# The first loads of a spline-built feed-forward layer: two sets of control points asked for by ScalarE, and x asked for behind the first set and its table

## The chip, the cores and the metric

One core of a Trainium2 chip runs the whole program. TensorE (PE, with its weight loads PEld), VectorE (DVE), ScalarE (ACT) and GpSimd (POOL) compute; SyncE (SP) here only asks for transfers. Each engine works through its own instructions in the order in which they were built, and stops at an instruction whose semaphores have not been reached. Transfers are asked for by an instruction on an engine's queue and then done by 16 DMA engines. The metric is the device time of one execution in microseconds (us).

## The reference

The input x is 4 sequences of 512 rows with 512 columns. Three steps follow each other: a feed-forward layer, an attention layer with a recurrent state, and the same feed-forward layer again. Only the first concerns the change. Its three weight matrices are not inputs: each is interpolated from a short vector of control points.

```python
def spline_reconstruct(control_points, out_size, in_size):
    n = out_size * in_size
    idx, f = _catmull_rom_grid(control_points.shape[0], n)
    p0, p1, p2, p3 = (control_points[idx[0]], control_points[idx[1]], control_points[idx[2]], control_points[idx[3]])
    ...
    w = 0.5 * (2.0 * p1 + (p2 - p0) * f + (2.0 * p0 - 5.0 * p1 + 4.0 * p2 - p3) * f2 + (3.0 * p1 - p0 - 3.0 * p2 + p3) * f3)
    return w.reshape(out_size, in_size)
gate_w = spline_reconstruct(gate_cp, INTER, HIDDEN)      # 2048 x 512
up_w = spline_reconstruct(up_cp, INTER, HIDDEN)          # 2048 x 512
down_w = spline_reconstruct(down_cp, HIDDEN, INTER)      # 512 x 2048
gate = jnp.einsum('bsh,ih->bsi', hidden_states, gate_w)
up = jnp.einsum('bsh,ih->bsi', hidden_states, up_w)
inter = jax.nn.silu(gate) * up
return jnp.einsum('bsi,hi->bsh', inter, down_w)
...
x = x + 0.5 * _L0_ffn_ref(_layernorm(x, axis=-1), ...)
x = x + _L0_attn_ref(_layernorm(x, axis=-1), ...)
x = x + 0.5 * _L0_ffn_ref(_layernorm(x, axis=-1), ...)
```

## The kernel before

The kernel never builds the dense weights. A row of a weight is piecewise cubic, so it keeps a small set of coefficients (`wc` for gate and up, `wr`, `we` and `cm` for down) and multiplies them with features of x. The first call of `ffn` (L299) has two pieces of work at its start that do not depend on each other:

- **Features of the first sequence.** `load` (L331) brings x, 1 MB, into the tile `ffn_x`. `whole` (L384) normalizes it: statistics on VectorE (`ln_st`, `ln_mv`, `ln_var`), the power -0.5 on GpSimd (`ln_rstd`, L346), the scaled rows on VectorE (`ln_xn`, L361). TensorE turns them (`ln_pt`, L368), ScalarE copies them (`ffn_xnT`, L369), TensorE multiplies them with the table `lag` (`pf`, L374), and ScalarE copies the eight results (`ft`, L378).
- **Coefficients.** `spline_weights` (L655) reads control points into the windows `win`: for each of gate, up and down 16 transfers of overlapping rows (L676), 6.5 KB each for gate and up, 3.1 KB for down. It also loads two tables of 1.5 MB (`tab`, L679 and L684) and constants (`shift`, `node`, `post`, `postd`, `rest`, `postr`, `sel`, `side`). `gate_up` (L712) first selects rows (`wr`, L707 and L709; one instruction covers gate and up together), then multiplies with the first table (`pr`, L719: gate's four on VectorE, up's four on GpSimd), and VectorE adds (`cf`, L720). TensorE turns the sums (`cf_pt`, L725), ScalarE copies them (`nat`, L726), and three engines permute them into `cfT` (L731). `down` (L741) does the like with the second table (`pr` L749, `cfd` L750, `cf_pt` L753, `natd` L755) and permutes into `cfTd` with 32 small copies on GpSimd (L766).

Then comes `hidden` (L427) for the first sequence: 16 products for gate (`pg`) and 16 for up (`pu`, L439). The coefficients are finished on the way, by `block` (L769): every second step a pair of `pw` products (L777) from `cfT`, a copy (L780) and a predicated copy (L781) into `wc`, and at every step `pwd` products (L789) from `cfTd` and a small table `rw` that SyncE brings. `pw`, `pwd`, `pwe`, `pf`, `ln_pt` and `cf_pt` share two PSUM buffers. Two further sequences are loaded meanwhile (`ffn_x`, L608 and L615) and their statistics taken.

In this part nothing fixes the order of the work by hand. The tile framework orders each engine's instructions when the kernel is built, from its own estimates of when each will be ready; so a moved transfer can change the order on other engines too. The later parts (`by_hand`, L604, and the attention) are ordered by hand.

All transfers except GpSimd's gathers of `hid` (L458) are asked for by SyncE, in one queue. The framework gives the completion of transfers eight semaphores in turn: an instruction that asks for a transfer waits until the transfer eight places earlier, on the same semaphore, has landed.

The lines that set the order of the first asks are L398 and L399 (x, then `lag`), then, inside `spline_weights`, `shift`, gate's 16, the first table, up's 16, down's 16, and the constants.

Of the kernel before, what the change touches and what calls it, by code (L numbers as in the profile page):

```python
# [19 lines left out]
P = 128  # L20
# [31 lines left out]
G_LAG = G_NODE + NG_F * 2 * P  # L52
G_POST = G_LAG + NC * NG_F * NODES
# [211 lines left out]
def tile_macaron(ctx, tc, x, w_qkvz, w_ba, conv_w, dt_bias, a_log, norm_w, w_out, cps, consts, grid, starts, out):  # L265
    nc = tc.nc
# [32 lines left out]
    def ffn(src, dst, build, beside=iter(())):  # L299
        with ExitStack() as st:  # L300
# [3 lines left out]
            io = pool(early, "ffn_io", 2)  # L304
# [4 lines left out]
            ps = pool(late, "ffn_ps", 2, space=PSUM, side="right")  # L309
            py = pool(late, "ffn_py", 1, space=PSUM, side="right")  # L310

            lag = wp.tile([P, NC, NG_F * NODES], F32, name="lag")
            wc = [wp.tile([P, 2, GR], F32, name=f"wc{g}", tag=f"wc{g}") for g in range(NG_F)]
# [17 lines left out]
            def load(b, name, pool):  # L331
                xt = pool.tile([P, NT, H], F32, name=name)
                nc.sync.dma_start(xt, src(b).rearrange("(t p) h -> p t h", p=P))
                return xt
# [49 lines left out]
            def whole(xt):  # L384
                ft, stats, norms, turns, inter = features(xt)
                stats()
                for n_, t_ in zip(norms, turns):
                    n_()
                    t_()
                    tick()  # L390
                drain()
                for f in inter:
                    f()
                    tick()
                drain()
                return ft

            xt = load(0, "ffn_x", io)  # L398
            nc.sync.dma_start(lag.rearrange("p c k -> p (c k)"), grid[:, G_LAG:G_POST])  # L399
            built = ExitStack()  # L400
            if build:
                with ExitStack() as scratch:
                    coefficients, block = spline_weights(built, scratch, wc, ps)
                    ft = whole(xt)
                    for f in coefficients:
                        f()
            else:
                for g in range(NG_F):
                    nc.sync.dma_start(wc[g].rearrange("p m i -> p (m i)"), wg_d[g])
                ft = whole(xt)  # L410
# [16 lines left out]
            def hidden(b, ft):  # L427

                to, box = hid[b % 2], {}

                def gate(k):
                    if build and b == 0:
                        block(k, wr, we, cm)
                    product(k, 0)

                def product(k, m):
                    at = (k % 2) * P
                    pm = box[m] = gu.tile([P, S], F32, name=("pg", "pu")[m], tag="gu")
                    nc.tensor.matmul(pm, wc[k // 2][:, m, at : at + P], ft[k // 2], start=True, stop=True)  # L439
                    if m:  # L440
                        pg = box[0]
                        later(1, lambda: finish(k, pg, pm))

                def finish(k, pg, pu):
                    sg = wk.tile([P, S], F32, name="ffn_sg")
                    nc.scalar.activation(sg, pg, AF.Silu)
                    it = wk.tile([P, S], F32, name="ffn_it", bufs=4)
                    nc.vector.tensor_tensor(it, pu, sg, ALU.mult)  # L448
                    nc.sync.dma_start(to[k * P : (k + 1) * P, :], it)

                return [f for k in range(NB) for f in (lambda k=k: gate(k), lambda k=k: product(k, 1))]
# [155 lines left out]
            if B > 1:  # L607
                xt = load(1, "ffn_x", io)  # L608
                plan["nxt"] = features(xt)
                plan["nxt"][1]()  # L610
            if build:
                first = hidden(0, plan["ft"])
# [39 lines left out]
                    if step is None:  # L652
                        break

    def spline_weights(st, scratch, wc, ps):  # L655

# [8 lines left out]
        win = [c1.tile([P, 2, NB, ext[0]], F32, name="win0"), c1.tile([P, 1, 4, ext[1]], F32, name="win1")]  # L667
        for m in range(3):
            n = m // 2
            r = ext[n] - 9  # L670
            rows = 512 // r

            for q in range(16):
                view = bass.AP(cps[m].tensor, starts[n][q], [[r, rows], [1, ext[n]]])
                first = (q * rows) % P
                nc.sync.dma_start(win[n][first : first + rows, m % 2, q * rows // P, :], view)  # L676
            if m == 0:
                tab = [c1.tile([P, 64 * NF * NJ], F32, name=f"tab{k}", tag=f"tab{k}") for k in range(2)]
                nc.sync.dma_start(tab[0], grid[:, G_TAB[0] : G_TAB[1]])  # L679
        node = sp.tile([64, NG_F, 2, P], F32, name="node")  # L680
        nc.sync.dma_start(node.rearrange("p g e j -> p (g e j)"), grid[:64, G_NODE:G_LAG])
        post = sp.tile([P, INTER // 4], F32, name="post")
# [127 lines left out]
                nc.sync.dma_start(we_d, we)  # L810
                nc.sync.dma_start(cm_d, cm.rearrange("p c h -> p (c h)"))

        return (gate_up, down), block

# [893 lines left out]

    steps = attention()
    ffn(lambda b: x[b], lambda b: x1[b], True, steps)
    for _ in steps:
        pass
    ffn(lambda b: x2[b], lambda b: out[b], False)


# [30 lines left out]
```

## Time and profile before

| | us |
|---|---|
| median of 4 runs | 3772.76 |
| lowest, highest | 3770.35, 3775.47 |
| the profiled execution | 3773.43 |
| its span on the core | 3771.6 |
| PE busy | 3553.8 (94%) |
| DVE busy | 2543.2 (67%) |
| ACT busy | 1469.4 (39%) |
| POOL busy | 866.2 (23%) |

The profile is of one execution. All times in it count from the start of the span. "Busy" sums the instructions of an engine; asking for a transfer and waiting for a semaphore are not counted. In a timeline a line gives the start, the busy time, the engine, the source line, the operation, what it writes and reads, the shapes, and in brackets how long the engine had been idle and what ended that. "SPq" is SyncE's queue of asks. A "DMA" piece in the chain of work is the time from the ask to the landing. The windows table gives for each stretch the busy time of each engine and the clock that TensorE was granted as a share of full speed.

### The profile page before, as it was taken

What the parts mean: (1) busy time and instruction counts of PE and PEld (TensorE: products, weight loads), DVE (VectorE), ACT (ScalarE), POOL (GpSimd) and SP (SyncE); (2) the same over time, 40 slices, a digit from 0 to 9 for tenths busy, and PEclk for the clock granted to TensorE, in tenths of its full rate; (3) what the DMA queues carried; (4) which work ended last, traced back from release to release, by engine and by line L of the source; (5) the groups of instructions that cost most, each with busy time, mean ns of one, the idle gap of its engine ahead of it and who ended that gap; (6) DMA issues with size and microseconds to landing.
All of it is one profiled execution on the core that took longest, in us unless ns stands there. A gap on an engine that the chain in (4) does not pass through costs nothing.

```text
span 3771.6 us, 62529 instructions
## 1 busy us (share of the span) xinstructions
PE 3553.8 (94%) x24568; PEld 1966.2 (52%) x24568; DVE 2543.2 (67%) x5928; ACT 1469.4 (39%) x3440; POOL 866.2 (23%) x655
## 2 busy tenths in 40 slices
PE   5998679999999999999999999999999999987998
PEld 2333245555555555555555556555555555553333
DVE  5223677787777788778777777777778777552321
ACT  2321124444444444444444444444444444443221
POOL 2113112222222222222222222222222221210221
PEclk8999889999999999999999999999999999998999
DMA  4435311212222222122222222222222211203452
GB/s 144 154 131 187 104 47 48 71 58 62 66 70 64 82 64 72 55 60 65 63 60 82 60 71 61 60 61 65 73 82 60 63 52 51 66 22 111 151 199 90
DMA packets 303093, 302.25 MB, mean 80 GB/s; under 512 B 96880, under 2 KB 231312, under 8 KB 302224
## 3 DMA queue, kind: packets, MB, share of 16 engines
q1 hardware_dynamic: 292560, 264.70, 22.6%
q0 software_dynamic: 10240, 33.56, 2.9%
q8 instruction: 194, 3.18, 0.4%
q14 instruction: 99, 0.81, 0.1%
HBM read 247.60 MB, written 50.59 MB: 79 GB/s over the span
## 4 chain that ended last, share of the span: by engine, by line
PE 70%; DVE 15%; POOL 5%; ACT 5%; DMA 3%; issue 2%; SPq 1%; DVEq 0%; POOLq 0%; ACTq 0%
PE pj L1041 15%; PE py L1507 12%; PE pz L1359 9%; DVE acc L1051 4%; PE pks L1398 4%; PE y L492 3%; PE pp L1283 3%; PE pg L439 3%; PE pu L439 3%; PE pos L1436 3%; POOL oo L1480 2%; DVE ee L1227 2%; PE pzz L1423 2%; PE pu L1344 2%; PE pos L1434 2%
## 5 line engine op out<-in xcount | busy, mean ns | idle before, releaser
L1051 DVE SCALAR_TENSOR_TENSOR acc<-pj,cw,acc 128x511 f32<-128x511 f32 (+2 forms) x768 | 574.3, 748 | 188.8 <-ACT acc L1049 170.6
L1041 PE MATMUL pj<-xnT,w_v 128*128 128x512 f32 x1024 | 521.0, 602 | 0.0
L1359 PE MATMUL pz<-w_z,xnT 128*128 128x512 f32 x1024 | 514.2, 614 | 0.0
L1507 PE MATMUL py<-w_o,gT 128*128 128x512 f32 x1024 | 509.5, 611 | 0.4
L448 DVE TENSOR_TENSOR ffn_it<-pu,ffn_sg 128x512 f32<-128x512 f32 x128 | 88.4, 691 | 362.2 <-PE pu L439 250.8
L1041 PE MATMUL pj<-xnT,w_q 128*128 128x512 f32 x512 | 255.9, 603 | 9.4 <-ACT ksq L1112 9.4
L1041 PE MATMUL pj<-xnT,w_k 128*128 128x512 f32 x512 | 247.1, 602 | 3.9 <-DVE acc L1051 3.3
L1415 ACT ACTIVATE tq<-pks,rqe 128x128 f32<-128x128 f32 x384 | 120.0, 363 | 330.5 <-DVE rq L1256 192.5
L1485 ACT ACTIVATE oo<-oo,orr 128x128 f32<-128x128 f32 x512 | 162.6, 389 | 204.6 <-POOL oo L1480 204.6
L1082 POOL TENSOR_TENSOR rsk<-msk,phalf 128x4 f32<-128x4 f32 x64 | 66.8, 1044 | 719.3 <-DVE msk L1080 712.1
L1049 ACT ACTIVATE acc<-pj,cw 128x512 f32<-128x512 f32 x256 | 175.1, 684 | 139.1 <-PE pj L1041 139.1
L1507 PEld LDWEIGHTS py<-w_o,gT 128*128 128x128 f32 x1024 | 170.3, 190 | 107.5 <-issue 96.4
L1359 PEld LDWEIGHTS pz<-w_z,xnT 128*128 128x128 f32 x1024 | 170.3, 191 | 101.4 <-issue 90.4
L1082 POOL TENSOR_TENSOR rsq<-msq,phalf 128x4 f32<-128x4 f32 x64 | 64.9, 1014 | 681.3 <-DVE msq L1080 668.6
L1059 ACT ACTIVATE th<-acc 128x512 f32<-128x512 f32 x256 | 161.7, 632 | 148.2 <-DVE acc L1051 144.1
L1041 PEld LDWEIGHTS pj<-xnT,w_v 128*128 128x128 f32 x1024 | 170.5, 191 | 70.7 <-issue 64.1
L1221 POOL TENSOR_TENSOR ee<-ident,w 128x1024 f32<-128x1024 f32 x64 | 141.3, 2208 | 226.1 <-DVE pT L1292 226.1
L458 POOL DMA_INDIRECT nat<-hid,idx x128 | 122.9, 960 | 299.7 <-PE y_pt L509 104.5
L1473 DVE TENSOR_REDUCE om<-osq 128x4 f32<-128x512 f32 x128 | 87.1, 680 | 153.8 <-ACT osq L1472 153.8
L1166 DVE TENSOR_TENSOR inv<-inv,inv_tmp 128x30 f32<-128x30 f32 (+14 forms) x480 | 168.9, 352 | 16.5
L1479 POOL TENSOR_TENSOR orr<-om,phalf 128x8 f32<-128x8 f32 x64 | 104.9, 1640 | 311.9 <-DVE om L1477 311.9
L1423 PEld LDWEIGHTS pzz<-rr,tt 128*128 128x128 f32 x768 | 114.5, 192 | 114.5 <-DVE rr L1408 49.2
(213 smaller groups left out, 6824.1 us busy)
## 6 DMA issues: line engine op xcount, KB each, us to landing
hid<-ffn_it SPq DMA_DIRECT2D x128, 256.0 KB, 2.1
w_v<-in_L_attn_W_qkvz SPq DMA_DIRECT2D x64, 512.0 KB, 3.6
w_z<-in_L_attn_W_qkvz SPq DMA_DIRECT2D x64, 512.0 KB, 5.1
ab<-decay_c SPq DMA_DIRECT2D x64, 512.0 KB, 3.7
w_o<-in_L_attn_W_out SPq DMA_DIRECT2D x32, 1024.0 KB, 5.6
w_k<-in_L_attn_W_qkvz SPq DMA_DIRECT2D x64, 256.0 KB, 2.8
w_q<-in_L_attn_W_qkvz SPq DMA_DIRECT2D x64, 256.0 KB, 3.2
ad<-decay_b SPq DMA_DIRECT2D x256, 32.0 KB, 2.2
```

The source lines that it names most:

```text
L439: nc.tensor.matmul(pm, wc[k // 2][:, m, at : at + P], ft[k // 2], start=True, stop=True)
L1041: nc.tensor.matmul(pj, w()[:, c, col : col + DK], xnT[:, c, :], start=c == 0, stop=c == NC - 1)
L1049: nc.scalar.activation(acc, pj, AF.Copy, scale=cw[:, ch, 3:4])
L1051: nc.vector.scalar_tensor_tensor(acc[:, d:], pj[:, : S - d], cw[:, ch, 3 - d : 4 - d], acc[:, d:], ALU.mult, ALU.add)
L1059: nc.scalar.activation(th, box["acc"], AF.Tanh)
L1166: nc.vector.tensor_tensor(ee[:, j + 1 :, :j], ee[:, j + 1 :, :j], tj, ALU.add)
L1221: nc.gpsimd.tensor_tensor(ee, id8, bc(s["w"], 3, P), ALU.mult)
L1359: nc.tensor.matmul(pz, xnT[:, c, t * P : (t + 1) * P], pair["wz"][:, c].rearrange("p j k -> p (j k)"), start=c == 0, stop=c == NC - 1,)
L1398: nc.tensor.matmul(pks[:, j].rearrange("p r v -> p (r v)"), m[:, tok], box["state"].rearrange("p r v -> p (r v)"), start=True, stop=True,)
L1423: nc.tensor.matmul(pzz[:, r], s["tT"][:, 2 * t + r], rr[:, r], start=True, stop=True)
L1485: nc.scalar.activation(s["oo"][:, t, r], s["oo"][:, t, r], AF.Copy, scale=s["orr"][:, u : u + 1])
L1507: nc.tensor.matmul(box["py"], pair["gT"][r][:, t, :], pair["wo"][:, r, :], start=r == 0, stop=r == 3)
```

## The change

The load of x and of `lag` becomes a function, `first`. When coefficients are built, `spline_weights` calls it after gate's 16 transfers and the first table have been asked for. The 16 transfers of up and the 16 of down are asked for by ScalarE's queue (`nc.scalar`) in place of SyncE's. In the second call of `ffn`, which builds nothing, `first` is called at the place where the two loads stood.

```diff
-            xt = load(0, "ffn_x", io)
-            nc.sync.dma_start(lag.rearrange("p c k -> p (c k)"), grid[:, G_LAG:G_POST])
+            def first():
+                xt = load(0, "ffn_x", io)
+                nc.sync.dma_start(lag.rearrange("p c k -> p (c k)"), grid[:, G_LAG:G_POST])
+                return xt
+
             built = ExitStack()
             if build:
                 with ExitStack() as scratch:
-                    coefficients, block = spline_weights(built, scratch, wc, ps)
+                    coefficients, block, xt = spline_weights(built, scratch, wc, ps, first)
                     ft = whole(xt)
                     for f in coefficients:
                         f()
             else:
+                xt = first()
...
             for q in range(16):
                 view = bass.AP(cps[m].tensor, starts[n][q], [[r, rows], [1, ext[n]]])
-                first = (q * rows) % P
-                nc.sync.dma_start(win[n][first : first + rows, m % 2, q * rows // P, :], view)
+                at = (q * rows) % P
+                eng = nc.scalar if m else nc.sync
+                eng.dma_start(win[n][at : at + rows, m % 2, q * rows // P, :], view)
             if m == 0:
                 tab = [c1.tile([P, 64 * NF * NJ], F32, name=f"tab{k}", tag=f"tab{k}") for k in range(2)]
                 nc.sync.dma_start(tab[0], grid[:, G_TAB[0] : G_TAB[1]])
+                xt = first()
...
-        return (gate_up, down), block
+        return (gate_up, down), block, xt
```

In the built program the order of instructions differs before the second group's `pw` and nowhere behind it. What moves beside the asks themselves: VectorE and GpSimd select rows and start `pr` ahead of the statistics of x, which stand among the `pr` and `cf` steps; `cfT`'s copy on VectorE stands behind the statistics of the next x; the first `wc` predicate stands behind three `ln_xn` of that x; `pwd`, `pg`, `pwe` and `pu` of the first group stand behind both `pw`; and the first two `rw` are asked for ahead of the first store of `wc`. ScalarE's 32 asks stand ahead of its first table load.

More of the change, by code (lines that the diff above doesn't have):

```diff
@@ L653, in ffn, with spline_weights @@
                         break
-    def spline_weights(st, scratch, wc, ps):
+    def spline_weights(st, scratch, wc, ps, first):
         sp = st.enter_context(tc.tile_pool(name="spl", bufs=1))
```

## The prediction, made before the result was known

> **What bounds the kernel now.** Over the whole span it is TensorE (PE busy 94%, 70% of the chain that ended last). I read the 40 slices first: PE is not full in the first two (5 and 9 tenths; the very first 94 us), and the diff touches nothing behind them. So next came the chain that ended last, for the first 75 us:
>
> ```profile
> 1.64 6.22 DMA lag<-in_grid
> ...
> 12.49 0.04 issue
> 12.53 6.39 DMA tab<-in_grid
> 18.95 0.33 SPq L676
> 19.27 0.04 issue
> 19.32 0.43 SPq L676
> ...
> 31.78 8.23 DMA tab<-in_grid
> ```
>
> The chain runs through SyncE's queue: an ask for 6.5 KB of control points costs 0.43 + 0.04 = 0.47 us, and 48 stand in one row. An ask also waits until the one eight places ahead has landed (18.95 is the landing of the table asked for at 12.53). My yardstick is the second group's `pw` (L777), whose weight loads start at 69.37. Behind it every engine's instruction order is the same in both builds, so what is won or lost there reaches the end. The timeline up to it:
>
> ```profile
> 24.76 0.46 DVE L707 TENSOR_TENSOR wr<-win,shift 128x288 f32<-128x288 f32 x1 [11.61 <-DMA win<-in_L_ffn_down_cp]
> ...
> 29.07 3.36 DVE L719 TENSOR_TENSOR pr<-wr,tab 128x768 f32<-128x768 f32 x2
> ...
> 40.33 0.95 DVE L720 TENSOR_REDUCE cf<-pr 128x128 f32<-128x768 f32 x1 [0.99 <-POOL pr L719]
> 42.02 0.95 DVE L720 TENSOR_REDUCE cf<-pr 128x128 f32<-128x768 f32 x1 [0.75 <-POOL pr L719]
> ...
> 55.94 4.75 POOL L766 COPY cfTd<-natd 128x108 f32<-128x108 f32 x32 [4.06 <-ACT natd L755]
> ...
> 69.37 1.02 PEld L777 LDWEIGHTS pw<-cfT,node 32*128 32x128 f32 x8 [0.69 <-DVE cm L803]
> ```
>
> VectorE idles 11.61 us until up's last rows have landed, then works nearly without a break to 53.4. Last the table by 5 us windows (columns: PE, PEld, DVE, ACT, POOL busy, granted clock):
>
> ```profile
> 20.00:25.00 5.00, 3.01 (x28) 0.47 (x24) 0.24 (x1) 2.46 (x5) 0.00 (x0) 1.00 0.18 13
> 25.00:30.00 5.00, 0.00 (x0) 0.00 (x0) 4.72 (x11) 0.00 (x0) 0.88 (x1) 0.51 0.09 7
> ...
> 55.00:60.00 5.00, 4.68 (x9) 2.34 (x8) 2.14 (x5) 2.61 (x5) 4.07 (x27) 0.50 0.13 47
> 60.00:65.00 5.00, 5.00 (x24) 1.78 (x22) 3.16 (x8) 1.13 (x3) 0.69 (x6) 0.74 0.48 109
> ```
>
> TensorE's clock is halved once it has idled, and stays so for 7 us after it works steadily again (from 55.56; 0.74 over 60 to 65 means full from 62.6).
>
> **The change, step by step**, in us from the span's start.
>
> *1. The queues.* SyncE: ident at 0.73, then shift and 16 gate asks, so the table is asked for at 0.73 + 18 x 0.47 = 9.2 (before 12.53) and, by the 6.39 of its row, lands at 15.6; I take 16.1, since ScalarE's small loads now move beside it. ScalarE asks from 0.73 on. No ask of ScalarE is in the trace: the bounds are SyncE's 0.43 and the 0.96 of a GpSimd gather (L458), and I take SyncE's 0.47, the same kind of ask; at 0.96 up would land at 16.9 and `pr` start 5.1 later, with the kernel 3.4 slower than before. Up's last is asked for at 7.8 and lands at 9.6 (1.8 for small loads); gate's at 10.5. L707 and L709 take 4.3 (24.76 to 29.07) and end at 15.2, so the table comes last: `pr` starts at 16.2, 12.9 earlier.
> What else is moved: x stands behind the table and, by the built order, waits for a landing of ScalarE's down rows; before, lag's half megabyte landed 1.4 behind x (6.50, 7.88), so x's megabyte behind the table is put at 19 to 20 (before 6.5). It is first needed at 21.2 (step 2); past that VectorE stops. lag lands by about 21, needed at 32.5. The second table waits for x, 19.5 + 6.4 and half a megabyte of node: 28, needed at 36.9. node, post and the side tables land before 31, the next two x by 38; nothing asks for them before 43.9. ScalarE's 32 asks hold up its own table load (1.28, before at 0.73) and its copies: six of down's asks stand behind the table's landing, so they end at 19 and the load at 20.3; its first copy is due at 29. All that is covered.
>
> *2. VectorE.* The layer norm of the first x was done in the idle 6.5 to 13.2; the built order now puts it among the `pr` and `cf` steps. It costs 3.1 for statistics (6.50 to 9.61) and 2.0 for four `ln_xn`. From 16.2: two `pr`, two reductions as before, 5.0, to 21.2; statistics 3.1 and four `pr` or reductions at 0.87 to 27.8; `ln_xn` from 28.0 (GpSimd's 1.0 for rstd lies beside the last of these); four of them with a reduction between to 30.9; two more reductions 32.6; GpSimd's last `pr` (1.74) starts when its buffer is free at 31.8, its reduction ends at 34.5. Down: 2.4 + 2.6 + 4.4 (rows 42.89 to 53.41, without the `cfT` copy of 1.1, which now comes later): 43.9 against 53.41. Of 12.9 there are 9.5 left.
>
> *3. TensorE.* Before, `pf` was done at 23.0, 20 us before anything behind it was ready. Now it cannot start before the last `ln_xn`, turn and copy (30.9 + 0.95 + 0.6): 32.5, and `cf_pt` stands behind it. It takes 7.24 (15.77 to 23.01) at full clock. TensorE has idled until 28, so part is at half: none at the least (first burst: 1.00 in 10 to 15), 7 us at the most (second burst); I take 5, nearer the second, which also followed a long idle: 9.7, end at 42.2. The transposes and their copies take 4.2 as before: 46.4; down's transposes and `natd` 47.4, before 55.9: 8.5 left.
> Trainium skill, "TensorE: Matmul & The Clock Gate", Part 1, says that one busy window of about 3.4 us frees the clock. By that the half-clock part here is 3.4 and the end 0.8 earlier; the row of 55.56 to 62.6 says twice that.
>
> *4. GpSimd.* `cfT` 2.4 to 48.8, the 32 copies 4.75 to 53.6. In the built order rstd of the next x follows (1.0), three `ln_xn` wait for it, and the first `wc` predicate stands behind those: 54.6 + 1.5 + 0.75 + 0.44 = 57.3. Its PSUM buffer is what `pwd` needs: 57.4, before 63.69: 6.3 left.
>
> *5. The first group.* From `pwd` to the second group's `pw` it took 63.69 to 69.37 = 5.7. But before, `pg`, `pu`, `pg`, `pu` were already done in the wait for `cfTd`; now they stand behind `pwd`: 4 x 0.98 = 3.9 at full clock. Against that the idle 65.39 to 67.23, a wait for rstd, goes: 1.8. So 7.8, and 2.5 for 5 us at half clock: 10.3. Second `pw` at 67.7: 1.7 earlier than 69.37.
>
> The profiled execution (3773.43 us: span 3771.6, 1.8 around it) would be 3771.7. It lies 0.7 above the median of the runs, 3772.76, so the median becomes 3771.1.
>
> Trainium skill, "DMA: Bandwidth & Descriptors", Issuing engines are not separate DMA queues, speaks against the change: a second issuing engine saves only the sequencer's issue time, usually small. Here the issue is 0.47 for a 1.8 us landing. If only up's 16 asks, 7.5 us, were saved in step 1, 5.4 of its 12.9 would be missing and the kernel 3.7 slower, 3776.5.
>
> **Rivals.**
> *A. The clock is free at once*, faster. Steps 3 and 5 without half clock (2.5 each), the table at 15.6 (0.5), `cf_pt` 0.8 quicker: 1.7 + 6.3 = 8.0 earlier, 3764.8. For: the first burst. Against: the second, and TensorE idle between `natd` and `pw`.
> *B. The eight counters starve*, slower. Two queues now share the eight landing counters, so an ask waits for the fourth ahead on its own queue. At 1.8 us landing that is just free (4 x 0.47 = 1.88). At 3.0, the median of up's asks before, an ask takes 0.75 and the table comes 18 x 0.28 = 5.0 later: 3.3 slower, 3776.1. It decides from 2.26 us landing on (1.7 / 18 per ask); 3.9 us makes 7.5. Against: up's 3.0 came from the table ahead of it on the same queue.
> *C. Nothing is gained*: TensorE at half clock through all of `pf`, 4.8 later in step 3: 3.1 slower, 3775.9. The saved waiting is then paid back by work that was free before.
>
> **How the numbers follow.** A measurement of this kernel can tell about 0.2%, 7.5 us, from no change. Forecast 0.50; A 0.22; C 0.15; B 0.13, of which 0.07 with landings past 3.9 us. Faster by over 0.2%: A, 0.22. Slower: 0.07. Within: 0.50 + 0.15 + 0.06 = 0.71. The range holds A and goes 1.3 beyond it (3763.5), and B at 3.0 us, the dear ask of step 1 (3776.2) and C, with 1.3 more (3777.5); past these lie landings near 3.9 us and runs that add several of the small terms.
>
> **What will show it.** Step 1: the first `pr` near 16 with the table as its releaser, ScalarE's queue asking at 0.47. Step 2: cfd's last reduction near 44. Step 3: `pf` from 32.5, granted clock 0.5 for about 5 us. Step 4: `pwd` near 57. Step 5: second `pw` near 67.7. Wrong if small landings exceed 2.3 us, if x is late for VectorE's statistics, if the clock stays halved past 62, or if the time moves behind 70 us, where the order is the same.

## The result, and the profile after

The changed kernel takes 3770.43 us (median of 40 runs, 3763.76 to 3779.63), the kernel before 3773.33 us (median of 60 runs). The ratio is 0.9991, 95% interval 0.9987 to 0.9996: 2.9 us less by the medians, 1.5 to 4.9 by the interval. Predicted were 3771.1 us and a change within 0.2%. The profiled execution has a span of 3769.8 us, against 3771.6.

The chain of work of the changed kernel, from its first 75 us:

```profile
9.00 2.32 DMA win<-in_L_ffn_up_cp
...
11.70 5.55 DMA win<-in_L_ffn_down_cp
17.25 0.02 issue
17.27 5.33 DMA ffn_x<-in_L_attn_x
22.59 0.02 issue
22.62 1.29 DVE ln_st L341 x2
...
35.70 9.71 PE pf L374 x64
...
49.42 5.66 POOL cfTd L772 x32
55.08 0.97 POOL ln_rstd L346
56.05 2.59 issue
58.65 1.08 PE pwd L795 x16
59.73 2.01 PE pg L443 x2
...
68.30 1.07 PE pw L783 x8
```

SyncE's asks are gone from the middle of it. In their place stand x (1 MB, asked for only when a row of down had landed), the layer norm, `pf`, and behind GpSimd's copies the `ln_rstd` of the next x. The timeline:

```profile
10.29 0.43 SPq L684 DMA_DIRECT2D tab<-in_grid  x1
...
17.00 3.36 DVE L725 TENSOR_TENSOR pr<-wr,tab 128x768 f32<-128x768 f32 x2 [0.61 <-DMA tab<-in_grid]
...
22.62 1.29 DVE L341 BATCH_NORM_STATS2 ln_st<-ffn_x 128x6 f32<-128x512 f32 x2 [0.54 <-DMA ffn_x<-in_L_attn_x]
...
44.69 1.80 DVE L756 TENSOR_REDUCE cfd<-pr 128x128 f32<-128x768 f32 x2
...
58.12 0.42 DVE L787 COPY_PREDICATED wc<-post,pw 128x256 f32<-128x256 uint8 x1
...
68.23 0.74 PEld L783 LDWEIGHTS pw<-cfT,node 32*128 32x128 f32 x8 [0.76 <-issue]
```

The first product starts 12.1 us earlier than before (29.07), the second group's `pw` only 1.1 earlier (69.37). Two more profiled executions of the same kernel (a0 and b1 below) have it at 65.76 and 66.23; of the kernel before there is one profile. The three together show where the 12 went (us; before first, then the mean of the three):

| stretch | before | changed | difference |
|---|---|---|---|
| first `pr` on VectorE | 29.07 | 16.7 | -12.4 |
| from there to the end of `cfd`'s last reduction | 24.3 | 29.6 | +5.3 |
| from there to the end of the last `cfTd` copy | 7.3 | 7.5 | +0.2 |
| from there to the second `pw` | 8.7 | 13.0 | +4.3 |
| second `pw` | 69.37 | 66.74 | -2.6 |

So 2.6 of 12.4 are left; the measured gain is 2.9, 1.5 to 4.9 by its interval. The experiments take up the two stretches that grew.

### The profile page after: what moved, and what is told of

Its sections match the earlier page's. It is cut to its first block, busy times and chain, and to the rows that moved or that the text cites. A ratio compares the mean times of both kernels' runs of the same rounds, so it can differ in the third digit from the quotient of the medians.

```text
span 3769.8 us, 62534 instructions
## 1 busy us (share of the span) xinstructions
PE 3551.9 (94%) x24568; PEld 1964.0 (52%) x24568; DVE 2542.7 (67%) x5928; ACT 1470.6 (39%) x3440; POOL 866.6 (23%) x655
## 4 chain that ended last, share of the span: by engine, by line
PE 71%; DVE 14%; POOL 5%; ACT 5%; DMA 2%; issue 2%; ACTq 0%; DVEq 0%; POOLq 0%; SPq 0%
PE pj L1047 15%; PE py L1513 12%; PE pz L1365 9%; DVE acc L1057 4%; PE pks L1404 4%; PE y L496 3%; PE pg L443 3%; PE pp L1289 3%; PE pu L443 3%; PE pos L1442 2%; POOL oo L1486 2%; DVE ee L1233 2%; PE pzz L1429 2%; PE pu L1350 2%; PE pos L1440 2%
## 5 line engine op out<-in xcount | busy, mean ns | idle before, releaser
L1429 PEld LDWEIGHTS pzz<-rr,tt 128*128 128x128 f32 x768 | 114.5, 192 | 114.5 <-DVE rr L1414 49.2
```

The lines of the kernel that those rows point to most:

```text
L1429: nc.tensor.matmul(pzz[:, r], s["tT"][:, 2 * t + r], rr[:, r], start=True, stop=True)
```

## The experiments

Each experiment ran in one of three groups, beside the kernel before: a0, e5, e6 and e7, where that takes 3773 us as in the result; b1, b2, b3 and c1, where it takes 3826; and e1 to e4, where it takes 3831. Why it takes longer in two of them is open. The extra time lies behind the first 130 us: there b1 is 0.5 us behind a0, the same program, and at 150 us 9 us. So marks in the head can be compared across the groups, and times only by the ratio to the kernel before in the same group. e1 to e4 had no changed kernel beside them; for e3 and e4 the runs b1, b2 and b3 make up for it. Ratio and interval are the record's; the ratio can lie 0.0004 beside the quotient of the medians. Marks are of one profiled execution each (us). "Copies" is the end of the last `cfTd` copy; in e4 and b3 `pwd` starts before that, with the rows already copied.

| run | first `pr` on VectorE | `cfd` ends | copies | `pwd` | second `pw` | ratio to before (95%) |
|---|---|---|---|---|---|---|
| before | 29.07 | 53.4 | 60.7 | 63.7 | 69.4 | 1 |
| changed | 17.0 | 46.5 | 55.1 | 58.6 | 68.2 | 0.9991 (0.9987 to 0.9996) |
| a0 changed again | 16.3 | 46.2 | 53.1 | 56.7 | 65.8 | 0.9989 (0.9980 to 0.9998) |
| b1 changed, third | 16.8 | 46.2 | 53.1 | 56.7 | 66.2 | 0.9986 (0.9977 to 0.9995) |
| e1 queue only | 32.4 | 53.6 | 60.9 | 61.5 | 66.5 | 0.9983 (0.9974 to 0.9991) |
| e2 order only | 30.1 | 54.5 | 61.8 | 64.0 | 69.7 | 0.9999 (0.9991 to 1.0008) |
| e3 up only | 16.1 | 47.4 | 53.6 | 55.8 | 60.2 | 0.9971 (0.9961 to 0.9982) |
| b2 up only, again | 16.6 | 47.2 | 53.3 | 55.6 | 59.9 | 0.9975 (0.9964 to 0.9986) |
| e4 x on GpSimd's queue | 20.9 | 45.3 | 53.4 | 52.6 | 60.2 | 0.9969 (0.9957 to 0.9982) |
| b3 the same, again | 20.8 | 45.2 | 53.2 | 52.4 | 59.4 | 0.9974 (0.9964 to 0.9984) |
| e5 copies split | 16.2 | 45.9 | 52.1 | 55.2 | 64.2 | 0.9980 (0.9971 to 0.9989) |
| e6 TensorE kept busy | 16.3 | 46.2 | 53.1 | 56.7 | 65.3 | 0.9999 (0.9990 to 1.0008) |
| e7 rstd later | 16.7 | 46.5 | 54.8 | 55.8 | 64.9 | 0.9987 (0.9978 to 0.9996) |
| c1 up only, copies split | 16.4 | 46.7 | 50.7 | 54.8 | 59.1 | 0.9979 (0.9970 to 0.9988) |

The second `pw` is not a perfect yardstick. Where the clock is halved again just behind it, the lead changes: e3 is 9.2 us ahead of the kernel before at its second `pw` and 7.4 at the third group's (weight loads from 69.06 and 76.41), with a granted clock of 0.80 from 60 to 65 us; e2 goes from 0.3 behind to 2.0 behind, with 0.68 from 70 to 75.

**The changed kernel again (a0, b1).** No edit.

> The changed kernel once more, unedited, beside the next three on the same chip: 3 below before (ratio 0.9991), second pw near 68.2.

> The changed kernel a third time, beside the next three on one chip: 2.5 to 3.5 below before; its second pw moves between 65.8 and 68.2 with the place of the clock's windows.

Medians 3770.36 against 3772.96, and 3822.28 against 3825.85. The gain is small in both, as expected; a0's second `pw` was not near 68.2 but at 65.8. The head of one program moves by 2.5 us between executions, and most of it is the clock: `natd` starts 1.85 earlier in a0. The timeline of the first profile of the changed kernel, then of a0:

```profile
48.59 0.60 ACT L761 ACTIVATE natd<-cf_pt 128x512 f32<-128x512 f32 x1
```

```profile
46.74 0.60 ACT L761 ACTIVATE natd<-cf_pt 128x512 f32<-128x512 f32 x1 [0.97 <-PE cf_pt L759]
```

In a0 TensorE waits there for VectorE's sums; in the first profile `pf` and what stands behind it end later than those. The windows table of that first profile (columns: PE, PEld, DVE, ACT, POOL busy, granted clock, DMA share, GB/s; a clock of 1.00 in a stretch with no change recorded yet says nothing):

```profile
30.50:33.91 3.41, 2.65 (x12) 2.29 (x13) 3.41 (x6) 1.17 (x2) 0.42 (x1) 1.00 0.87 275
33.91:37.32 3.41, 2.73 (x14) 1.11 (x16) 2.34 (x5) 1.17 (x2) 1.75 (x1) 1.00 0.96 333
37.32:40.74 3.42, 3.42 (x20) 0.69 (x16) 2.84 (x10) 1.17 (x2) 1.16 (x1) 1.00 0.93 341
40.74:44.15 3.41, 3.41 (x36) 0.59 (x28) 2.05 (x3) 2.24 (x4) 3.07 (x2) 1.00 0.00 0
```

and of a0:

```profile
30.95:34.37 3.42, 3.40 (x16) 3.00 (x16) 3.42 (x6) 1.63 (x3) 0.22 (x1) 1.00 0.49 151
34.37:37.78 3.41, 2.73 (x26) 0.58 (x24) 2.25 (x6) 1.80 (x4) 1.53 (x1) 1.00 1.01 381
```

Read the count of matmuls beside the busy time. In the first profile 20 fill 3.42 us just before 40.74 and 36 fill it just after: the clock came free there, behind the first window that was full. In a0 a window happens to begin with the burst, is full (3.40 of 3.42), and from 34.37 on 26 matmuls take 2.73 us. So `ln_pt` and `pf` of the same program have 9.5 us at half clock (31.26 to 40.74) in one execution and 3.4 (30.97 to 34.37) in another.

**e1, the queue alone.** x and `lag` first on SyncE, as before; up and down on ScalarE.

```diff
+        xt = first()
         shift = c1.tile([P, G_TAB[0]], F32, name="shift")
...
                 nc.sync.dma_start(tab[0], grid[:, G_TAB[0] : G_TAB[1]])
-                xt = first()
```

> Only the queue is changed: up's and down's rows on ScalarE's queue, x and lag still first on SyncE's, then shift, gate, table. My theory (the layer norm of x, moved onto VectorE's and TensorE's chain, gives the gain back): gate's asks still stall behind x and lag, table lands near 21.5, first product pr starts near 21.5 (29.07 before, 17.0 in the changed kernel); but the layer norm and pf stay in the idle time ahead, so from pr to the second group's pw it takes 40.3 as before: second pw near 62, 7.5 earlier than before, time near 3766. Rival 1 (the gain comes from the order, the second queue only saves issue time that is hidden): 3773, as before. Rival 2 (the second queue itself is all of the measured 2.9): 3770.4, as the changed kernel.

Measured: 3823.33 against 3830.53. The time fits the first theory, but the head does not: second `pw` at 66.5, not 62. The timeline of e1 says why:

```profile
27.10 0.25 DVE L713 TENSOR_TENSOR wr<-win,shift 128x84 f32<-128x84 f32 x1 [5.92 <-DMA win<-in_L_ffn_down_cp]
...
32.37 1.81 DVE L725 TENSOR_TENSOR pr<-wr,tab 128x768 f32<-128x768 f32 x2
```

In the built order a select step for down, whose rows landed late, stands ahead of the last steps for gate and up on VectorE, and the products wait with it. `cfd` then ends where it did before (53.6), and what the head won came behind the copies (5.6 in place of 8.7). The measured gain (0.09% to 0.26%, 3.4 to 9.9 us) is larger than the head's 2.9; the rest is not explained.

**e2, the order alone.** All rows stay with SyncE.

```diff
-                eng = nc.scalar if m else nc.sync
+                eng = nc.sync
```

> Only the order is changed: shift, gate and the table ahead of x and lag, but all rows asked by SyncE. My theory: table asked at 9.2, x and lag behind it land near 21 and 22, up's asks wait for the landings eight places back and the last is asked near 25.5, lands 27.3, pr near 31.7 (29.07 before): second pw about 2.6 later than before, 3776. Rival (the order is what gains, the table comes 3.3 earlier): 3770.

Measured: 3830.90 against 3830.53, no change. In the timeline of e2 up's 16 asks take 13.39 us, because they wait for the landings of the table, x and `lag`:

```profile
10.73 13.39 SPq L681 DMA_DIRECT2D win<-in_L_ffn_up_cp  x16
...
30.13 3.39 DVE L725 TENSOR_TENSOR pr<-wr,tab 128x768 f32<-128x768 f32 x2
```

`pr` is 1.1 later than before (2.6 expected). The rival, that the order gains by itself, is out.

**e3 and b2, up alone on ScalarE's queue.** Down's rows go back to SyncE, behind x and `lag`.

```diff
-                eng = nc.scalar if m else nc.sync
+                eng = nc.scalar if m == 1 else nc.sync
```

> As the changed kernel, but down's rows go back to SyncE, behind x and lag, so that x doesn't wait for a landing of down's. My theory: x is asked near 10.8 in place of 17.3 and lands 1 to 2 earlier than 22.6; VectorE's statistics and all behind them start that much earlier; the built order also puts the first wc predicates ahead of the layer norm of the next x, so pwd comes 1.4 to 3 earlier. Second pw 65 to 67 (68.2 in the changed kernel), time 3767 to 3769.5. Rival (x's landing isn't on the path, the products are): 3770.4, no change against the changed kernel; and slower, 3772 or more, if down's 32-partition rows then come late for cfd.

> Up alone on ScalarE's queue once more, now beside the changed kernel. By the first run (second pw 60.2, 8 earlier than the changed kernel's 68.2): 9 below before and 6 below the changed kernel. If the gain of the first run belonged to that chip: within 2 of the changed kernel.

Measured: 0.9971, and 0.9975 (3817.85) beside the changed kernel's 0.9986 (3822.28) in the same group: 4.4 below it by the medians, 6 expected. The first run is better than expected, and only one of the two reasons expected holds: the statistics start at 21.1 in place of 22.6, but `cfd` ends no earlier (47.4 and 47.2 against 46.2 to 46.5). The gain is all in the order behind the copies, where e3 needs 6.6 us to the second `pw` and the changed kernel 13.0. The timeline of e3:

```profile
48.81 4.76 POOL L772 COPY cfTd<-natd 128x108 f32<-128x108 f32 x32 [1.64 <-ACT natd L761]
...
49.93 0.44 DVE L787 COPY_PREDICATED wc<-post,pw 128x256 f32<-128x256 uint8 x1 [2.50 <-ACT wc L786]
...
50.43 2.07 PE L443 MATMUL pg<-ft,wc 128*128 128x512 f32 x2
...
55.84 0.76 PE L795 MATMUL pwd<-cfTd,rw 128*32 128x128 f32 x16
...
60.20 1.76 PE L783 MATMUL pw<-cfT,node 32*128 32x256 f32 x8 [0.25 <-DVE cm L809]
```

The built order has the first `wc` predicate at 49.93 (58.12 in the changed kernel); `pg` and `pu` run beside the copies and a second `pg` right behind them, all ahead of `pwd`. In the kernel before, too, the predicate and these products stand ahead of `pwd`; the changed kernel lost that.

**e4 and b3, the first x on GpSimd's queue.**

```diff
             def first():
-                xt = load(0, "ffn_x", io)
+                xt = early_x
...
+            if build:
+                early_x = io.tile([P, NT, H], F32, name="ffn_x")
+                nc.gpsimd.dma_start(early_x, src(0).rearrange("(t p) h -> p t h", p=P))
+            else:
+                early_x = load(0, "ffn_x", io)
```

> As the changed kernel, but the first x is asked at the start by GpSimd's queue, so that its layer norm falls in VectorE's idle time again. My theory (what was given back is the layer norm and pf on the path): x lands near 8, layer norm before or beside the shift steps, pr near 18, from there 40.3 to the second pw as before: near 58.5 to 60, time 3762 to 3764. Rival 1 (the end is set by GpSimd's copies and the first group, not by the layer norm): less than 2 better than the changed kernel, 3769. Rival 2 (x's megabyte delays the control-point rows on the same rings): pr later than 20 and 3766 or more.

> First x on GpSimd's queue once more, now beside the changed kernel. By the first run (second pw 60.2): 9 below before, 6 below the changed kernel. If the gain of the first run belonged to that chip: within 2 of the changed kernel.

Measured: 0.9969, and 0.9974 (3816.02) beside the changed kernel's 0.9986 (3822.28), 6.3 below it by the medians. Both the theory and rival 2 hold in part. The rows are delayed beside x's megabyte, and `pr` starts at 20.9, which is past rival 2's 20. But the layer norm is then done, and from `pr` to the end of `cfd` e4 needs 24.4 us, as before (24.3), against 29.6 in the changed kernel. So the layer norm on VectorE's path costs 5.2. The order of the first group is better here too (from the copies 6.9), so the time alone does not separate the two. The timeline of e4:

```profile
20.93 3.36 DVE L731 TENSOR_TENSOR pr<-wr,tab 128x768 f32<-128x768 f32 x2
...
43.54 1.81 DVE L762 TENSOR_REDUCE cfd<-pr 128x128 f32<-128x768 f32 x2
...
47.92 0.44 DVE L793 COPY_PREDICATED wc<-post,pw 128x256 f32<-128x256 uint8 x1 [1.29 <-ACT wc L792]
```

**e5, the copies split.** The 32 `cfTd` copies go to GpSimd and VectorE in turn.

```diff
+                    turn_ += 1
+                    eng = (nc.gpsimd, v)[turn_ % 2]
...
-                    nc.gpsimd.tensor_copy(bass.AP(cfTd.tensor, ...), frm)
+                    eng.tensor_copy(bass.AP(cfTd.tensor, ...), frm)
```

> The changed kernel with the 32 cfTd copies dealt in turn to VectorE and GpSimd in place of GpSimd alone. My theory (GpSimd's copies, 49.4 to 55.1, hold up rstd, ln_xn, the first wc predicate and so pwd): the copies end about 2.5 earlier and pwd and the second pw come 2 to 3 earlier, 65.5 to 66: 2 to 3 below the changed kernel. Rival (TensorE's half clock sets the first group, pw ends at 54.9 anyway): less than 1 below.

Measured: 3765.51, 4.9 below a0 beside it (3770.36), 3.4 by the ratios. From `natd` to the last copy it takes 4.4 in place of 6.4. VectorE's 16 take 1.72 and GpSimd's 3.62, but 1.19 of this is one small copy that ran beside VectorE's copy into `cfT`; without such a meeting, in c1, the 16 take 1.64 and 2.59. The timeline of e5:

```profile
48.47 3.62 POOL L774 COPY cfTd<-natd 128x10 f32<-128x10 f32 x16
49.27 1.15 DVE L737 COPY cfT<-nat 64x1088 f32<-64x1088 f32 x1
49.28 1.19 POOL L774 COPY cfTd<-natd 128x2 f32<-128x2 f32 x1
50.34 1.72 DVE L774 COPY cfTd<-natd 128x108 f32<-128x108 f32 x16
```

The third line is one of the 16 in the first. The copies are on the path, as the prediction's fourth step had them. The median moved by more than the 2 to 3 expected. The two intervals overlap, and the built order moved as well: two `ln_xn` of the next x stand ahead of the first predicate in place of three.

**e6, TensorE kept busy.** Six products that nobody reads, on x as it lands.

```diff
+            def warm(n, of):
+                pm = gu.tile([P, S], F32, name="warm", tag="gu")
+                for _ in range(n):
+                    nc.tensor.matmul(pm, ident, of, start=True, stop=True)
...
                 xt = first()
+                warm(6, xt[:, 0, :])
```

> The changed kernel with six extra 128x128 by 128x512 products on TensorE, whose result nobody reads, that wait for x and so keep TensorE busy from 22.6 to about 31; every engine's order is otherwise the same. If half clock in ln_pt and pf is what TensorE's step costs: turns and pf at full clock, pf ends near 43 in place of 45.4, natd 1.5 earlier (cfd's last reduction, 46.4, then comes last), second pw 1.5 to 1.7 earlier, near 66.6: 1.5 below the changed kernel. Rival A (the clock alone is what was given back): 5 or more below it. Rival (VectorE's products set natd, TensorE is beside the path): no change, and 0.3 above it where the last product ends behind the first ln_xn.

Measured: 3771.20, 0.8 above a0 (0.9999 against 0.9989 by the ratios, with overlapping intervals). `ln_pt` and `pf` ran at full clock (`pf` from 34.56, 7.24 us), yet `natd` starts at 46.72, as in a0 (46.74) and b1 (46.69): `cfd`'s last reduction ends at 46.2 in all three and comes last. The half clock in `pf` costs nothing in such executions, and 1.9 in the first profiled one, where `natd` starts at 48.59. The rival that the clock was most of what was given back is out. The small gain of 1.5 that was expected did not come.

**e7, rstd of the next x later.** A wait is added so that `ln_xn` of the next x cannot stand ahead of the first `wc` predicates; TensorE's order stays.

```diff
-                plan["nxt"][1]()
+                if not build:
+                    plan["nxt"][1]()
...
+                    if i == 0 and B > 1:
+                        half = sm.tile([P, NT], F32, name="half", bufs=1)
+                        nc.vector.tensor_scalar(half, wr[:, 0, :NT], 0.0, -0.5, ALU.mult, ALU.add)
+                        plan["nxt"][1](half)
```

> The changed kernel with the exponent of the next x's rstd read from a tile that VectorE writes (one 128x4 operation, 0.1) behind the first wr predicate, so that rstd and three ln_xn of the next x can't stand ahead of the first wc predicates; TensorE's order stays. My theory (the predicate behind ln_xn delays pwd from 55.7 to 58.65): pwd near 55.7 and the second pw near 65.3, 3 below the changed kernel. Rival (the first group is bound by TensorE at half clock and by its order, in which pg, pu stand behind pwd): pwd early, but second pw less than 1.5 earlier.

The timeline of e7:

```profile
55.27 0.44 DVE L792 COPY_PREDICATED wc<-post,pw 128x256 f32<-128x256 uint8 x1 [1.94 <-ACT wc L791]
...
55.81 1.08 PE L800 MATMUL pwd<-cfTd,rw 128*32 128x128 f32 x16 [0.94 <-issue]
...
64.87 0.74 PEld L788 LDWEIGHTS pw<-cfT,node 32*128 32x128 f32 x8 [0.76 <-issue]
```

`pwd` follows the copies (54.8) by 1.0 in place of 3.6, and from the copies to the second `pw` it takes 10.1 in place of 13.0: 2.9 of the stretch are the wait behind `ln_xn`. The rest of the distance to e3 (6.6) is put down to TensorE's order: in e7 `pg` and `pu` still stand behind `pwd`. No run changes that order alone. The median is 3769.70, only 0.7 below a0, with an interval that holds both 3 and 0: by time the run does not decide.

**c1, up alone and the copies split.**

> Both edits that gained: up alone on ScalarE's queue, and the cfTd copies dealt to VectorE and GpSimd. If they add (GpSimd's copies 1.2 to 2 shorter behind the same natd): second pw 58 to 59, 10 to 12 below before. If the first group is then held by TensorE (pg, pu, pg at half clock ahead of pwd): as up alone, 9 below before.

Measured: the earliest second `pw` of all (59.1), but 3818.86 against 3825.85, 0.9979 and no better than b2 beside it. TensorE holds the group: the copies ended at 50.71, and `pwd` waits behind `pg`, `pu`, `pg`, as the timeline of c1 shows. The rival expectation is the nearer one.

```profile
50.62 2.07 PE L443 MATMUL pg<-ft,wc 128*128 128x512 f32 x2 [0.44 <-DVE wc L789]
...
54.84 0.64 PE L797 MATMUL pwd<-cfTd,rw 128*32 128x128 f32 x16
```

Over all runs the gain in time agrees with the lead at the second `pw` in sum: the nine edited kernels of the table (repeats averaged) have it 48 us earlier together, and 53 us less time (one minus the ratio, times before's median in that group). A single kernel can be 4 us off either way: e1 gained more than its head, e6 less.

## Why the prediction was right

**Step 1, the queues: right, 0.1 to 0.8 off in the end.** The table was asked for at 10.29, not 9.2, and `pr` started at 17.0, 16.3 and 16.8 in place of 16.2. An ask on ScalarE's queue costs what it costs on SyncE's, so the dear end of that bound is out. This line sums up ScalarE's 16 asks for up in the changed kernel (shortest, median and longest in ns, first and last start); SyncE's for gate have a median of 430.

```profile
L681 ACTq DMA_DIRECT2D win<-in_L_ffn_up_cp x16: 334/442/463, 0.7 to 9.0; - x16
```

What was late is rival B's mechanism in a small dose: the rows in the chain landed 2.0 to 2.6 after their ask in place of 1.8 (2.32 is one of them), and the four that may be under way on each queue then hold up the next. B priced 5 us; it was 1.1. x landed at 22.59, not 19 to 20, because down's row that it waits for was behind the table (the 5.55 in the chain), and VectorE stood still for 0.54. Two of the prediction's signs of being wrong, landings over 2.3 us and x late for the statistics, thus showed, both in small.

**Step 2, VectorE: right in kind, too cheap by 2.6.** The layer norm came onto the path; `cfd` ended at 46.5, not 43.9. Of this 0.8 came with `pr`, 0.5 with x, and 1.4 from the first `ln_xn`, put at 0.5 like the others. It took 1.97: the trace has it from 29.24 to 31.21, and a product of GpSimd from 29.20 to 30.92.

```profile
L361 DVE TENSOR_SCALAR ln_xn<-ffn_x,ln_mv,ln_rstd x4: 530/532/1970, 29.2 to 32.9; 128x512 f32<-128x512 f32 x4
```

This is the line's own summary in the changed kernel (shortest, median and longest of the four in ns, first and last start). GpSimd's timeline at that place:

```profile
29.20 1.72 POOL L725 TENSOR_TENSOR pr<-wr,tab 128x768 f32<-128x768 f32 x1
```

**Step 3, TensorE: right in the first profiled execution, by two errors that cancel in part.** `pf` began at 35.7 (32.5 predicted, late by step 2 and by the turns at half clock) and took 9.7 with 5.0 us of it at half clock, both as predicted. Behind it, the transposes and copies to `natd`'s end took 3.8 in place of 5.2. In a0 and b1 `pf` took 7.24, and `natd` was set by `cfd`. The rule of the Trainium skill, "TensorE: Matmul & The Clock Gate", Part 1 (one busy window of about 3.4 us frees the clock), held in a0. In the changed kernel's first profile it holds only if windows that were 0.78 and 0.80 busy do not count as busy: they freed nothing, the full one behind them did. In the profile of before it did not hold: the window from 55.80 to 59.21 was full and the clock came free only at 62.62.

**Step 4, GpSimd: right in sum.** Copies, rstd, `ln_xn`, predicate, `pwd`: 9.4 from `natd`'s end (49.2) to `pwd` (58.6), predicted 10.0. e5 and e7 show both halves of it on the path. Within it two terms were off and offset each other: GpSimd's part of `cfT` took 0.7 in place of 2.4, and the 32 copies took 5.7 in place of 4.75, since one of them took 1.12 (the longest before: 0.37). It ran beside VectorE's copy into `cfT`, which the built order had put there. From the changed kernel, the sum of the copies (shortest, median and longest in ns) and VectorE's copy:

```profile
L772 POOL COPY cfTd<-natd x32: 179/189/1122, 49.4 to 54.9; 128x1 f32<-128x1 f32 x12, 128x10 f32<-128x10 f32 x6, 128x2 f32<-128x2 f32 x4, 128x108 f32<-128x108 f32 x2
...
49.82 1.19 DVE L737 COPY cfT<-nat 64x1088 f32<-64x1088 f32 x1
```

**Step 5, the first group: right.** From `pwd` to the second `pw` 9.1 to 9.6, predicted 10.3. e3 agrees with the reason given, `pg` and `pu` behind `pwd`: where they stand ahead of it, it is 4.4.

The path was right: the wait at the queue goes, the layer norm, `pf` and the first group's order come onto the chain and take most of it back. That the sum came so near is in part luck: in the first profile it is made of errors of +0.8 (the table), +1.9 (x and the first `ln_xn`) and +0.5 (the turns) up to `pf`, and -1.4, -0.6 and -0.7 in the pieces behind it. For the second `pw` it gave 67.7; the three executions have 68.2, 65.8 and 66.2. The term that was mis-sized is the half clock of step 3: it was taken as 5 us of `pf` in every execution, and it is 5 in one and none in two. In that one the lead at the second `pw` is 1.1, in the others 3.6 and 3.1, 2.6 in the mean. e5 and e7, whose `pf` starts alike, have it too (9.3 and 9.4 us long), so how often it comes is open. It is the first part of rival A, which was priced at 8: its quicker `cf_pt` came true as well (3.3 in place of 4.2, in a0 too), its earlier table and its first group at full clock did not.

The prediction also held that what is won at the second `pw` reaches the end, because the order behind it is the same. In sum over the runs it does; for a single execution it does not (the last section).

The rule of the Trainium skill, "DMA: Bandwidth & Descriptors", Issuing engines are not separate DMA queues, by which a second engine saves only the sequencer's time, would have made it 3776.5 by the prediction's estimate, which counted up's own 16 asks (7.5 us). Here up's last rows landed at 11.3 in place of 24.4. Up's first ask went out at 0.73 in place of 13.01: 21 asks had stood ahead of it, 9.9 us at 0.47 each, and SyncE had waited 2.1 among them for x and `lag` to land. So most of it was the sequencer's time, as the rule has it; "usually small" did not fit a row of 48 asks.

## What to carry to other kernels

When the wait at the front of a kernel is removed, count the work that was done inside it, and price it on the engine that becomes the path: here 5.3 of 12.4 us were given back while the layer norm of x came onto VectorE's path (5.2 by e4). Then compare the built order of every engine behind the wait as well; 4.3 us more were lost behind the copies, where a planner, given other arrival times, put the next x ahead of the first predicate (2.9 by e7) and `pg` and `pu` behind `pwd`, and putting down's rows back on SyncE undid it. The best versions here are the small edit e3 and x on GpSimd's queue, 0.25% to 0.31% below the kernel before against 0.09% to 0.14% for the change itself; beside each other the intervals (0.9964 to 0.9986 and 0.9964 to 0.9984 against 0.9977 to 0.9995) overlap.

## What was not expected of the hardware

- An `ln_xn` on VectorE that meets a GpSimd product waits for nearly all of it: 1.97 us in place of 0.53. VectorE's reductions do not: two took 0.94 each beside another such product (from 20.28, GpSimd busy from 17.05 to 21.97). It goes the other way too: GpSimd's small copy took 1.12 beside VectorE's copy into `cfT`. Trainium skill, "SBUF — State Buffer", Who interferes with whom, says that VectorE and GpSimd share a pair of ports, that some VectorE instructions (`copy` and `tensor_scalar` among them) can take it, and that whoever issues first holds it for the whole instruction while the other is blocked. The trace agrees: `ln_xn` ran from 29.24 to 31.21, GpSimd's product having started at 29.20 and ended at 30.92.
- TensorE's clock can differ by 6 us of half speed between executions of one program (free after 9.5 and after 3.4 us of the same work).
- Behind the second `pw`, where the order is the same in both builds, the distance between two executions does not stay what it was (the prediction had this among its signs of being wrong). The lead of 1.1 us that the changed kernel's profile has at the second `pw` is 3.4 us at 200 us and 1.8 at the end. The windows table of the kernel before has a stretch at half clock behind an idle one:

```profile
160.00:165.00 5.00, 1.43 (x3) 0.43 (x4) 0.00 (x0) 0.00 (x0) 0.00 (x0) 1.00 0.65 236
165.00:170.00 5.00, 5.00 (x20) 1.52 (x18) 0.00 (x0) 0.60 (x1) 0.00 (x0) 0.66 0.00 0
```

and the changed kernel's has none there:

```profile
160.00:165.00 5.00, 3.23 (x16) 1.16 (x20) 0.00 (x0) 0.60 (x1) 0.00 (x0) 1.00 0.26 97
165.00:170.00 5.00, 5.00 (x32) 1.16 (x24) 0.69 (x1) 0.59 (x1) 0.00 (x0) 1.00 0.31 72
```

One profile can place the cause of a few us, but not measure what they come to in time; for that it took the repeated runs.
